# A graph-network stack on one core: min tiles on GpSimd in place of sums, all other tiles on ScalarE, products in column groups

## The chip, the cores and the metric

The kernel runs on one core of a Trainium2 chip. The time is the device time of that core in microseconds, the median of several executions. The profile is of one execution of its own. Engines are named as the profile names them: PE (TensorE matmuls), PEld (its weight loads), DVE (VectorE), ACT (ScalarE), POOL (GpSimd) and SP (SyncE).

## The reference, cut to what matters

Four layers follow each other on 64 independent graphs of 256 nodes with 128 features each, all in float32; one 256 x 256 matrix `adj` serves as adjacency and as weights. Each layer takes `h = relu(layernorm(x))` and adds its result to `x`: five steps of a gated recurrence, a two-hop polynomial filter, a normalised graph convolution, and an attention layer. The attention layer is what the change is about:

```python
W1, W2 = (W[:, :F], W[:, F:])                 # W is adj
s1 = jnp.einsum('bkf,ef->bke', x, W1)
s2 = jnp.einsum('bkf,ef->bke', x, W2)
pre = s1[:, :, None, :] + s2[:, None, :, :] + b_lin
h = jnp.where(pre >= 0, pre, ALPHA * pre)      # ALPHA = 0.2
e = jnp.einsum('bije,e->bij', h, a) + bias     # bias is adj
attn = jax.nn.softmax(e, axis=2)
out = jax.nn.sigmoid(jnp.einsum('bij,bjf->bif', attn, x))
```

For each graph this asks for 256 x 256 x 256 values of `h`, reduced over the last axis with the weights `a`. The leaky relu is split into `0.2 * pre` and `0.8 * relu(pre)`. The first part is linear, and its half that depends on `i` alone drops out of the softmax; the other half is one matrix product. The second part has to be made element by element. It can be made as `relu(s1 + s2)`, or as `max(s2, -s1)`, which differs from it by `s1` and so by something that is constant in a row of the softmax; `-min(-s2, s1)` is the same value again.

## The kernel before

The graphs go in 32 pairs (`NB = 2`, `p`). Each pair has a front (`front`, all layers up to the projections of the attention layer), 64 slots of score work, and two tails (`tail`, softmax and output of 128 rows each).

In slot `n` the kernel works on four rows `i` of both graphs (rows `r`, `r+32`, `r+64`, `r+96` of one 128-row half `ic`), for each of the two halves `k` of the 256 features. It makes one tile per `k`: 128 features x (4 rows x 2 graphs x 256 nodes `j`). Then `scores(n)` multiplies both tiles on PE with a sliding window of the weights (`win`), so that row `r` of each 32-row group of a PSUM bank gets its sum; each tile takes four 512-wide matmuls, one in each of the four 32-column groups of the array. One such matmul is two instructions in the profile[...].

Who makes the tiles:

- `k = 0`: DVE, one `tensor_tensor` with `max` over the whole tile (`rl_v`, L620). It reads `s2a` in PSUM (`banks[0]`) and `s1n` (negated) in SBUF, both broadcast.
- `k = 1`, two slots of three (kind "g"): POOL adds `s2b` and `s1b` over the whole tile (`rl_g`, L608, in `make_sum`), and ACT then takes the relu in place (L625).
- `k = 1`, the third slot (kind "s"): ACT alone, eight relu activations of 128 x 256 with `s1b` as pointer bias (`rl_s`, L635), reading a copy of `s2b` in PSUM (`s2p`, `banks[1]`).

`make(n + 4)` issues the tiles of DVE and ACT four slots ahead of their scores, `make_sum(n + 7)` the sums seven slots ahead. Buffers: 5 for `rl_v`, 6 for `rl_g`, 2 for `rl_s`. At the first tile of a pair, `make` projects `s2a` anew into `banks[0]` on PE; this overwrites what the tiles of the pair before read.

The front's and the tail's operations run between the slots. They are generators that yield before each step, and `background(n)` takes steps from them by their due times. A planner keeps a clock for each engine: `ran(engine, us, *after)` books a price for every piece of work, and the prices decide where a step is put. `in_order` then fixes each engine's program order as it was issued. A front begins two pairs ahead of its slots. The front's products with features as the contracted axis come in two forms: `side_by_side` issues four matmuls with 32 weight columns each, one for each column group; `project_token` (L295) and the last product of `tail` (L564) use one matmul with all 128 columns. Norms take their statistics on DVE, invert the root on POOL (`inverse_root`, L253 and L254), negate and scale the mean there (L326, L327), and apply both on ACT (L331).

Of the kernel before, what the change touches and what calls it, by code (L numbers as in the profile page):

```python
# [19 lines left out]
ALPHA = 0.2  # L20
PE, DVE, ACT, POOL = ENGINES = (mybir.EngineType.PE, mybir.EngineType.DVE, mybir.EngineType.Activation, mybir.EngineType.Pool)
AHEAD = 4
SUM_AHEAD = 7
SLOTS = 64


# [1 line left out]
def kernel(  # L28
# [47 lines left out]

    nc = tc.nc  # L80
    B, N, D = x.shape
    NC = N // P
# [6 lines left out]
    relu_pool = ctx.enter_context(tc.tile_pool(name="relu", bufs=3))  # L89
    psum = ctx.enter_context(tc.tile_pool(name="psum", bufs=1, space=PSUM))  # L90
    banks = [psum.tile([P, NB * N], F32, name=f"bank{k}") for k in range(8)]
    s2a, s2p = (b.rearrange("p (b n) -> p b n", b=NB) for b in banks[:2])
    pes = banks[2:4]


# [3 lines left out]
    def ran(engine, us, *after):  # L99
        clock[engine] = max(clock[engine], 0.0, *after) + us  # L100
        return clock[engine] + SEEN[engine]
# [131 lines left out]
        nc.scalar.dma_start(acol[:, k:k + 1], a_vec[k * P:(k + 1) * P].rearrange("(p o) -> p o", o=1))  # L233
    win = const.tile([P, NE, 63], F32, name="win")
    nc.vector.memset(win, 0.0)
    a_rep = const.tile([P, NE, P], F32, name="a_rep")
    nc.vector.memset(a_rep, 1.0)
    nblin = const.tile([P, NE], F32, name="nblin")
    nc.vector.tensor_scalar(nblin, blin, -1.0, None, op0=OP.mult)
    for k in range(NE):  # L240
        nc.vector.tensor_scalar(win[:, k, 31:32], acol[:, k:k + 1], 1.0 - ALPHA, None, op0=OP.mult)
        nc.vector.tensor_scalar(a_rep[:, k, :], a_rep[:, k, :], acol[:, k:k + 1], None, op0=OP.mult)

    pt = bank([P, P], "pt")
# [44 lines left out]
    def project_token(pp, pairs):  # L289

        pp = by_token(pp)
        for b in range(NB):
            for c in range(NC):
                for k, (t, w) in enumerate(pairs):
                    nc.tensor.matmul(pp[:, b, c, :], t[:, b, c * P:(c + 1) * P], w,  # L295
                                     start=(k == 0), stop=(k == len(pairs) - 1))

    def feat(name, **kw):
        return work.tile([P, NB, N], F32, name=name, **kw)
# [7 lines left out]
    SHORT = dict(tag="short", bufs=14)  # L307


    PROJECT, MIX, TURN, PRODUCT, PRODUCTS = 0.86, 1.74, 0.69, 1.18, 2.99  # L310
    COPY, BIASED, TANH, ELEMENTS = 0.48, 0.58, 0.57, 0.61

    def norm(src, since, h):

        stats = work.tile([P, NB * NC, 6], F32, name="stats")
        mv = work.tile([P, NB * NC, 2], F32, name="mv")
        s, h = rows_of(src), rows_of(h)
        yield DVE, since
        for k in range(NB * NC):
            nc.vector.bn_stats(stats[:, k, :], s[:, k, :])  # L320
        for k in range(NB * NC):
            nc.vector.bn_aggr(mv[:, k, :], stats[:, k, :])
        t = ran(DVE, 1.04, since)
        yield POOL, t
        inverse_root(mv[:, :, 1], OP.add, LN_EPS)
        nc.gpsimd.tensor_scalar(mv[:, :, 0], mv[:, :, 0], -1.0, None, op0=OP.mult)  # L326
        nc.gpsimd.tensor_mul(mv[:, :, 0], mv[:, :, 0], mv[:, :, 1])  # L327
        t = ran(POOL, 1.6, t)
        yield ACT, t
        for k in range(NB * NC):  # L330
            nc.scalar.activation(h[:, k, :], s[:, k, :], AF.Relu, bias=mv[:, k, 0:1], scale=mv[:, k, 1:2])  # L331
        return ran(ACT, 1.54, t)
# [6 lines left out]
        spare.append([bank[0], t])  # L339
        return c, t  # L340

    KEPT = {"hT": dict(bufs=4), "hT3": {}, "s2b": {}}

    READY = {}

    def front(p):
# [160 lines left out]
        hT, t_hT = copied("hT3", b, t)  # L507
        yield PE, t_hT, 1
        b = take()
        project(b[0], adj_t[:, 1, P:2 * P], hT)  # L510
        t = ran(PE, PROJECT, t_hT, b[1])
        yield ACT, t
        s2b, t_2 = copied("s2b", b, t)
        yield PE, t_hT, 1
        b = take()
        project(b[0], adj_t[:, 0, P:2 * P], hT)
# [8 lines left out]
        project(b[0], adj_t[:, 0, 0:P], hT)  # L525
        t = ran(PE, PROJECT, t_hT, b[1])
        yield ACT, t
        s1n = feat("s1n")
        nc.scalar.activation(s1n, by_feature(b[0]), AF.Identity, bias=nblin[:, 0:1], scale=-1.0)
        t_n = ran(ACT, BIASED, t)  # L530
        spare.append([b[0], t_n])
        READY[p] = dict(x3=x3, h3=h3, hT=hT, s1n=s1n, s1b=s1b, s2b=s2b, t_b=max(t_b, t_2), t_n=t_n)

    def tail(p, ic, pe, since, x3, h3):

# [25 lines left out]
        po = b[0][:, :NB * D].rearrange("p (b d) -> p b d", b=NB)  # L561
        for k in range(NB):
            for c in range(NC):
                nc.tensor.matmul(po[:, k, :], wT[:, k, c, :], h3[:, k, c, :], start=(c == 0), stop=(c == NC - 1))  # L564
        t = ran(PE, PRODUCT, t, b[1])
        yield DVE, t_s
        rs = work.tile([P, NB], F32, name="rs")
# [15 lines left out]

    TILES = {}
    t_pe = {}
    t_free = {"v": [0.0] * 5, "g": [0.0] * 6, "s": [0.0] * 2}
    TAILED = set()

    def where(n):
        return n // SLOTS, n % SLOTS // 32, n % 32  # L590

    def kind(n):
        return "s" if n % 3 == 0 else "g"

    def operands(n, s1, s2):

        _, ic, r = where(n)
        i0 = ic * P + r
        whole = [P, 4, NB, N]
        rows = s1[:, :, i0:i0 + 97:32].rearrange("p b g -> p g b").unsqueeze(3)  # L600
        return s2.unsqueeze(1).to_broadcast(whole), rows.to_broadcast(whole)

    def make_sum(n):
        if n >= NPAIR * SLOTS or kind(n) != "g":
            return
        ops = READY[where(n)[0]]
        tile_ = relu_pool.tile([P, 4, NB, N], F32, name="rl_g", bufs=6)
        nc.gpsimd.tensor_add(tile_, *operands(n, ops["s1b"], ops["s2b"]))  # L608
        TILES[n, 1] = tile_, ran(POOL, 3.58, ops["t_b"], t_free["g"].pop(0))

    def make(n):
        if n >= NPAIR * SLOTS:
            return
        p, ic, r = where(n)
        ops = READY[p]
        if "t_2a" not in ops:
            project(banks[0], adj_t[:, 1, 0:P], ops["hT"])
            ops["t_2a"] = ran(PE, PROJECT, clock[DVE] + SEEN[DVE])
        tile_ = relu_pool.tile([P, 4, NB, N], F32, name="rl_v", bufs=5)
        nc.vector.tensor_tensor(tile_, *operands(n, ops["s1n"], s2a), op=OP.max)  # L620
        TILES[n, 0] = tile_, ran(DVE, 2.2, ops["t_2a"], ops["t_n"], t_free["v"].pop(0))
        if kind(n) == "g":
            tile_, since = TILES[n, 1]
            t = tile_.rearrange("p g b n -> p (g b n)")
            nc.scalar.activation(t, t, AF.Relu)  # L625
            TILES[n, 1] = tile_, ran(ACT, 1.8, since)
        else:
            if "t_2p" not in ops:
                nc.scalar.copy(s2p, ops["s2b"])
                ops["t_2p"] = ran(ACT, COPY, ops["t_b"])  # L630
            tile_ = relu_pool.tile([P, 4, NB, N], F32, name="rl_s", bufs=2)
            for g in range(4):
                for b in range(NB):
                    i = ic * P + g * 32 + r
                    nc.scalar.activation(tile_[:, g, b, :], s2p[:, b, :], AF.Relu,  # L635
                                         bias=ops["s1b"][:, b, i:i + 1], scale=1.0)
            TILES[n, 1] = tile_, ran(ACT, 2.86, t_free["s"].pop(0))

    def scores(n):
        p, ic, r = where(n)  # L640
        pe = pes[ic % 2]
        if r == 0:
            project(pe, g2, READY[p]["hT"], stop=False)
            ran(PE, PROJECT, t_pe.get(p * NC + ic - 2, 0.0))
        for k in range(NE):
            tile_, since = TILES.pop((n, k))

            for g in range(4):
                nc.tensor.matmul(pe[g * 32:(g + 1) * 32, :], win[:, k, 31 - r:63 - r], flat(tile_[:, g]),  # L649
                                 start=False, stop=(r == 31 and k == NE - 1), skip_group_check=True)  # L650
            t_free["v" if k == 0 else kind(n)].append(ran(PE, PROJECT, since))

    CHAINS = {}

# [37 lines left out]

    def background(n):
        p, k = n // SLOTS, n % SLOTS + 1
        room = SLOTS - SUM_AHEAD - 3
        while True:
            todo = []
            for key in CHAINS:
                if isinstance(key, tuple):
                    late = 2.0  # L700
                else:

                    due = total * (0.5 * (min(1.0, k / room) + 1) if key == p + 1 else 0.5 * k / SLOTS)
                    late = due - CHAINS[key][2]
                todo.append((-late, key))
            for late, key in sorted(todo, key=lambda x: x[0]):
                late = -late
                if late < -AHEAD_STEPS:
                    continue
                wait = wait_of(key)  # L710
                if wait <= TOLERANCE or late > LATE and wait < 100 or key == p + 1 and k >= room:
                    break
            else:
                return
            advance(key)

    AHEAD_STEPS, TOLERANCE, LATE = 15, 0.05, 8

    for n in range(SUM_AHEAD):
        make_sum(n)  # L720
    for n in range(AHEAD):
        make(n)
    in_order()
    for n in range(NPAIR * SLOTS):
        if n % SLOTS == 0:
            begin_front(n // SLOTS + 2)
        background(n)
        make_sum(n + SUM_AHEAD)
        make(n + AHEAD)
        scores(n)  # L730
        in_order()
        if n % 32 == 31:
            p, ic, _ = where(n)
            begin((p, ic), tail(p, ic, pes[ic % 2], clock[PE] + SEEN[PE], READY[p]["x3"], READY[p]["h3"]))
# [33 lines left out]
```

## Time and profile before

| | us |
|---|---|
| three runs | 5563.02, 5567.29, 5567.29 |
| median | 5567.29 |
| profiled execution, its own time | 5561.99 |
| span of the profiled execution | 5560.2 |
| first score matmul starts | 149.2 |
| last score matmul ends | 5549.3 |

Up to 149 us the kernel sets up its constants and runs the fronts of the first two pairs; the 2048 slots follow, and the last tail ends the program. Over the span PE is busy for 96%, DVE 95%, ACT 97% and POOL 94%; the mean granted PE clock is 0.989. DMA carries 25.9 MB at a mean of 5 GB/s.

A line of the page's groups has the line of the kernel, the engine, the operation, output and inputs by name with their shapes, the count, the busy time of the group, the mean nanoseconds of one, and the idle time of the engine just before them with what ended most of it. Consecutive instructions of an engine overlap, so the mean duration of one is longer than the distance from one start to the next. A line of the waits has the waiting engine, tile and line, what it waited for, the total microseconds, the number of times and the longest. A line of the timeline has start, length, engine, line, operation and count, merged over like instructions. "Seam" is used below for the place where the slots of one pair end and those of the next begin.

### The profile page before, as it was taken

The page shows a single profiled execution, that of the slowest core. Times are in us where ns is not written, and L with a number is a line of the kernel's source. Part 1 is how long each engine was busy: PE and PEld are TensorE (multiplying, and loading weights), DVE is VectorE, ACT ScalarE, POOL GpSimd, SP SyncE. Part 2 cuts the span into 40 slices and gives each one's busy share as a digit, 9 for nine tenths or more (in the row PEclk, how much of TensorE's full clock was granted, in tenths as well). Part 3 has the DMA queues.
Part 4 walks back from the last instruction along what each step waited for, and adds up shares of the span by engine and source line. Part 5 has one row for each costly group of instructions (what it writes and reads, how often), then busy time and mean ns, then how long its engine had stood idle before and what let it go on. Part 6 is the DMA issues. An engine that isn't in the chain of part 4 may idle for free.

```text
span 5560.2 us, 122022 instructions
## 1 busy us (share of the span) xinstructions
PE 5364.9 (96%) x51733; PEld 1876.4 (34%) x51733; DVE 5273.8 (95%) x4224; ACT 5390.2 (97%) x8910; POOL 5222.9 (94%) x2075
## 2 busy tenths in 40 slices
PE   7999999999999999999999999999999999999998
PEld 3333333333333333333333333333333333333322
DVE  3989999999999999999999999999999999999998
ACT  3999999999999999999999999999999999999998
POOL 1999999999999999999999999999999999999998
PEclk9999999999999999999999999999999999999999
DMA  0000000000000000000000000000000000000000
GB/s 20 2 4 5 5 2 5 5 4 5 4 3 5 4 5 5 2 5 5 4 5 4 3 5 4 5 5 2 5 5 4 5 4 3 5 2 3 3 2 4
DMA packets 38741, 25.91 MB, mean 5 GB/s; under 512 B 3504, under 2 KB 38192, under 8 KB 38192
## 3 DMA queue, kind: packets, MB, share of 16 engines
q1 hardware_dynamic: 35088, 17.05, 1.0%
q8 instruction: 404, 6.62, 0.5%
q10 hardware_dynamic: 3104, 1.05, 0.1%
q14 instruction: 145, 1.19, 0.1%
HBM read 9.70 MB, written 8.39 MB: 3 GB/s over the span
## 4 chain that ended last, share of the span: by engine, by line
PE 56%; DVE 20%; ACT 16%; issue 6%; POOL 2%; DMA 0%; ACTq 0%; DVEq 0%; POOLq 0%; SPq 0%
PE bank L649 35%; DVE rl_v L620 16%; PE bank L259 16%; ACT rl_g L625 7%; ACT rl_s L635 6%; POOL rl_g L608 2%; PE bank L295 2%; PE bank L287 2%; PE bank L564 1%; ACT h L331 1%; DVE bank L404 1%; PE bank L280 1%; DVE d L400 1%; DVE hT L408 1%; DVE stats L320 0%
## 5 line engine op out<-in xcount | busy, mean ns | idle before, releaser
L608 POOL TENSOR_TENSOR rl_g<-s2b,s1b 128x2048 f32<-128x2048 f32 x1365 | 4901.1, 3626 | 147.6 <-PE bank L649 133.5
L620 DVE TENSOR_TENSOR rl_v<-bank,s1n 128x2048 f32<-128x2048 f32 x2048 | 4576.9, 2280 | 151.9 <-PE bank L649 89.8
L625 ACT ACTIVATE rl_g<-rl_g 128x2048 f32<-128x2048 f32 x1365 | 2846.3, 2198 | 19.0 <-POOL rl_g L608 18.7
L635 ACT ACTIVATE rl_s<-bank,s1b 128x256 f32<-128x256 f32 x5464 | 2226.4, 730 | 41.2 <-PE bank L649 40.1
L649 PE MATMUL bank<-rl_v,win 128*32 128x512 f32 x16384 | 2187.9, 599 | 12.0 <-DVE rl_v L620 11.6
L649 PE MATMUL bank<-rl_g,win 128*32 128x512 f32 x10920 | 1434.4, 595 | 14.3 <-ACT rl_g L625 14.3
L649 PEld LDWEIGHTS bank<-rl_v,win 128*32 128x32 f32 x16384 | 514.1, 110 | 1068.2 <-issue 933.2
L649 PE MATMUL bank<-rl_s,win 128*32 128x512 f32 x5464 | 754.5, 595 | 0.5 <-ACT rl_s L635 0.5
L649 PEld LDWEIGHTS bank<-rl_g,win 128*32 128x32 f32 x10920 | 352.5, 111 | 858.4 <-issue 710.6
L649 PEld LDWEIGHTS bank<-rl_s,win 128*32 128x32 f32 x5464 | 190.2, 110 | 439.5 <-issue 374.2
L259 PE MATMUL bank<-adj_t,h 128*32 128x256 f32 x5120 | 309.5, 382 | 7.4 <-ACT h L419 7.4
L259 PE MATMUL bank<-hT,adj_t 128*32 128x512 f32 x1024 | 149.0, 662 | 105.4 <-DVE rl_v L620 104.6
L259 PEld LDWEIGHTS bank<-adj_t,h 128*32 128x32 f32 x5120 | 156.2, 110 | 156.0 <-ACT h L419 34.8
L331 ACT ACTIVATE h<-x,mv 128x128 f32<-128x128 f32 x384 | 166.5, 581 | 11.8 <-POOL mv L327 11.7
L259 PE MATMUL bank<-mT,w 128*32 128x512 f32 x1280 | 168.3, 592 | 0.0
L259 PE MATMUL bank<-mT,w5t 128*32 128x512 f32 x1280 | 168.3, 592 | 0.0
L259 PE MATMUL bank<-rh,u5t 128*32 128x512 f32 x1280 | 168.2, 592 | 0.0
L395 ACT ACTIVATE bank<-bank,gate_b 128x512 f32<-128x512 f32 x160 | 156.5, 978 | 11.6 <-PE bank L259 11.2
L259 PE MATMUL bank<-hT,u3t 128*32 128x512 f32 x1280 | 166.7, 593 | 0.0
L259 PE MATMUL bank<-mT,w4t 128*32 128x512 f32 x1280 | 166.7, 592 | 0.0
L377 ACT ACTIVATE bank<-bank,gate_b 128x512 f32<-128x512 f32 x160 | 152.1, 951 | 13.2 <-PE bank L259 13.0
L381 DVE SCALAR_TENSOR_TENSOR rh<-bank,hT 128x512 f32<-128x512 f32 x160 | 109.3, 683 | 56.7 <-ACT bank L377 55.7
(111 smaller groups left out, 3458.7 us busy)
## 6 DMA issues: line engine op xcount, KB each, us to landing
xin<-in_x_dram SPq DMA_DIRECT2D x64, 128.0 KB, 2.2
out_dram<-o SPq DMA_DIRECT2D x64, 128.0 KB, 1.8
w_raw<-in_L_gnn_w_w_dram ACTq DMA_DIRECT2D x3, 128.0 KB, 2.6
th_raw<-in_L_gnn_Theta_dram ACTq DMA_DIRECT2D x1, 320.0 KB, 3.3
adj_n<-in_adj_dram SPq DMA_DIRECT2D x1, 256.0 KB, 5.0
w_raw<-in_L_gnn_u_w_dram ACTq DMA_DIRECT2D x2, 64.0 KB, 2.2
bias<-in_L_gnn_bias_dram ACTq DMA_DIRECT2D x2, 64.0 KB, 3.4
w<-in_L_gnn_weight_dram ACTq DMA_DIRECT2D x1, 64.0 KB, 3.0
```

The costliest lines, as they stand in the source:

```text
L259: nc.tensor.matmul(o[g:g + 32], w[:, g:g + 32], t, start=start, stop=stop, skip_group_check=True)
L287: nc.tensor.transpose(pt[:, b, c, :], ht[:, b, c * P:(c + 1) * P], ident)
L295: nc.tensor.matmul(pp[:, b, c, :], t[:, b, c * P:(c + 1) * P], w, start=(k == 0), stop=(k == len(pairs) - 1))
L331: nc.scalar.activation(h[:, k, :], s[:, k, :], AF.Relu, bias=mv[:, k, 0:1], scale=mv[:, k, 1:2])
L377: nc.scalar.activation(r[0], pr[0], AF.Tanh, bias=br, scale=0.5)
L381: nc.vector.scalar_tensor_tensor(rh, by_feature(r[0]), 1.0, hT, op0=OP.add, op1=OP.mult)
L395: nc.scalar.activation(pv[0], pv[0], AF.Tanh, bias=bh, scale=1.0)
L608: nc.gpsimd.tensor_add(tile_, *operands(n, ops["s1b"], ops["s2b"]))
L620: nc.vector.tensor_tensor(tile_, *operands(n, ops["s1n"], s2a), op=OP.max)
L625: nc.scalar.activation(t, t, AF.Relu)
L635: nc.scalar.activation(tile_[:, g, b, :], s2p[:, b, :], AF.Relu, bias=ops["s1b"][:, b, i:i + 1], scale=1.0)
L649: nc.tensor.matmul(pe[g * 32:(g + 1) * 32, :], win[:, k, 31 - r:63 - r], flat(tile_[:, g]), start=False, stop=(r == 31 and k == NE - 1), s ...
```

## The change

GpSimd no longer makes sums. It makes whole tiles: for 5 of every 16 slots the `k = 1` tile is eight `tensor_scalar` instructions of 128 x 256 with `min` of `s2n` (the negated projection) and a pointer scalar out of `s1b`. All other `k = 1` tiles come from ScalarE, as eight relu activations with scale -1 on `s2n`. In one slot of 32 ScalarE makes the `k = 0` tile as well; in the others DVE makes it, now as `min` of `s1a` and the negated projection in `banks[0]`. Tiles made by `min` are multiplied with `win_n`, the window with its sign turned. Buffers are 5 for "v", 3 for "m" and 5 for "s". The products of `project_token` and of the tail go through `side_by_side`. The negation of the mean in `norm` moves from POOL to DVE. Four of the planner's prices change, and `M_US` is a new one.

```diff
-SUM_AHEAD = 7
+EARLY = 7
+M_OF_16, M_US = 5, 7.3
...
+    win_n = const.tile([P, NE, 63], F32, name="win_n")
+    nc.vector.memset(win_n, 0.0)
+    w2n = const.tile([P, N], F32, name="w2n")
+    nc.vector.tensor_scalar(w2n, adj_t[:, 1, :], -1.0, None, op0=OP.mult)
...
-    nblin = const.tile([P, NE], F32, name="nblin")
-    nc.vector.tensor_scalar(nblin, blin, -1.0, None, op0=OP.mult)
...
+        nc.vector.tensor_scalar(win_n[:, k, 31:32], acol[:, k:k + 1], ALPHA - 1.0, None, op0=OP.mult)
...
-                    nc.tensor.matmul(pp[:, b, c, :], t[:, b, c * P:(c + 1) * P], w,
-                                     start=(k == 0), stop=(k == len(pairs) - 1))
+                    side_by_side(pp[:, b, c, :], t[:, b, c * P:(c + 1) * P], w, k == 0, k == len(pairs) - 1)
...
-    PROJECT, MIX, TURN, PRODUCT, PRODUCTS = 0.86, 1.74, 0.69, 1.18, 2.99
+    PROJECT, MIX, TURN, PRODUCT, PRODUCTS = 0.86, 1.74, 0.69, 0.88, 2.64
...
-        t = ran(DVE, 1.04, since)
+        nc.vector.tensor_scalar(mv[:, :, 0], mv[:, :, 0], -1.0, None, op0=OP.mult)
+        t = ran(DVE, 1.12, since)
         yield POOL, t
         inverse_root(mv[:, :, 1], OP.add, LN_EPS)
-        nc.gpsimd.tensor_scalar(mv[:, :, 0], mv[:, :, 0], -1.0, None, op0=OP.mult)
         nc.gpsimd.tensor_mul(mv[:, :, 0], mv[:, :, 0], mv[:, :, 1])
-        t = ran(POOL, 1.6, t)
+        t = ran(POOL, 1.4, t)
...
-                nc.tensor.matmul(po[:, k, :], wT[:, k, c, :], h3[:, k, c, :], start=(c == 0), stop=(c == NC - 1))
+                side_by_side(po[:, k, :], wT[:, k, c, :], h3[:, k, c, :], c == 0, c == NC - 1)
...
-    def kind(n):
-        return "s" if n % 3 == 0 else "g"
+    def kind(n, k):
+        if k == 0:
+            return "s" if n % 32 == 7 else "v"
+        return "m" if n * M_OF_16 % 16 < M_OF_16 else "s"
...
-        nc.gpsimd.tensor_add(tile_, *operands(n, ops["s1b"], ops["s2b"]))
-        TILES[n, 1] = tile_, ran(POOL, 3.58, ops["t_b"], t_free["g"].pop(0))
+        for g in range(4):
+            for b in range(NB):
+                i = ic * P + g * 32 + r
+                nc.gpsimd.tensor_scalar(t[:, g, b, :], ops["s2n"][:, b, :], ops["s1"][1][:, b, i:i + 1], None, op0=OP.min)
+        TILES[n, 1] = t, ran(POOL, M_US, ops["t_1"][1], ops["t_2"], free)
...
-        if "t_2a" not in ops:
-            project(banks[0], adj_t[:, 1, 0:P], ops["hT"])
+        if "t_s2" not in ops:
+            project(banks[0], w2n[:, 0:P], ops["hT"])
+            nc.scalar.copy(s2[1], ops["s2n"])
...
-        nc.vector.tensor_tensor(tile_, *operands(n, ops["s1n"], s2a), op=OP.max)
...
-            nc.scalar.activation(t, t, AF.Relu)
-            TILES[n, 1] = tile_, ran(ACT, 1.8, since)
...
+            if kind(n, k) == "v":
+                nc.vector.tensor_tensor(t, *operands(n, ops["s1"][0], s2[0]), op=OP.min)
+                TILES[n, k] = t, ran(DVE, 2.2, since)
+            else:
+                for g in range(4):
+                    for b in range(NB):
+                        i = ic * P + g * 32 + r
+                        nc.scalar.activation(t[:, g, b, :], s2[k][:, b, :], AF.Relu,
+                                             bias=ops["s1"][k][:, b, i:i + 1], scale=-1.0)
+                TILES[n, k] = t, ran(ACT, 2.86, since)
...
-                nc.tensor.matmul(pe[g * 32:(g + 1) * 32, :], win[:, k, 31 - r:63 - r], flat(tile_[:, g]),
+                nc.tensor.matmul(pe[g * 32:(g + 1) * 32, :], w[:, k, 31 - r:63 - r], flat(t[:, g]),
```

`w` is `win` for tiles of kind "s" and `win_n` for the others. In `front`, `s2b` becomes `s2n` (projected with `w2n`), and `s1n` becomes `s1a` (bias `blin`, scale 1).

More of the change, by code (lines that the diff above doesn't have):

```diff
@@ L91 @@
     banks = [psum.tile([P, NB * N], F32, name=f"bank{k}") for k in range(8)]
-    s2a, s2p = (b.rearrange("p (b n) -> p b n", b=NB) for b in banks[:2])
+    s2 = [b.rearrange("p (b n) -> p b n", b=NB) for b in banks[:2]]
     pes = banks[2:4]
@@ L340, in copied @@
         return c, t
-    KEPT = {"hT": dict(bufs=4), "hT3": {}, "s2b": {}}
+    KEPT = {"hT": dict(bufs=4), "hT3": {}, "s2n": {}}
     READY = {}
@@ L509, in front @@
         b = take()
-        project(b[0], adj_t[:, 1, P:2 * P], hT)
+        project(b[0], w2n[:, P:2 * P], hT)
         t = ran(PE, PROJECT, t_hT, b[1])
         yield ACT, t
-        s2b, t_2 = copied("s2b", b, t)
+        s2n, t_2 = copied("s2n", b, t)
         yield PE, t_hT, 1
@@ L527, in front @@
         yield ACT, t
-        s1n = feat("s1n")
-        nc.scalar.activation(s1n, by_feature(b[0]), AF.Identity, bias=nblin[:, 0:1], scale=-1.0)
+        s1a = feat("s1a")
+        nc.scalar.activation(s1a, by_feature(b[0]), AF.Identity, bias=blin[:, 0:1], scale=1.0)
         t_n = ran(ACT, BIASED, t)
         spare.append([b[0], t_n])
-        READY[p] = dict(x3=x3, h3=h3, hT=hT, s1n=s1n, s1b=s1b, s2b=s2b, t_b=max(t_b, t_2), t_n=t_n)
+        READY[p] = dict(x3=x3, h3=h3, hT=hT, s1=(s1a, s1b), s2n=s2n, t_1=(t_n, t_b), t_2=t_2)
     def tail(p, ic, pe, since, x3, h3):
@@ L585 @@
     t_pe = {}
-    t_free = {"v": [0.0] * 5, "g": [0.0] * 6, "s": [0.0] * 2}
+    t_free = {"v": [0.0] * 5, "m": [0.0] * 3, "s": [0.0] * 5}
     TAILED = set()
@@ L600, in operands, with new_tile, make_early @@
         rows = s1[:, :, i0:i0 + 97:32].rearrange("p b g -> p g b").unsqueeze(3)
-        return s2.unsqueeze(1).to_broadcast(whole), rows.to_broadcast(whole)
-    def make_sum(n):
-        if n >= NPAIR * SLOTS or kind(n) != "g":
-            return
-        ops = READY[where(n)[0]]
-        tile_ = relu_pool.tile([P, 4, NB, N], F32, name="rl_g", bufs=6)
-        nc.gpsimd.tensor_add(tile_, *operands(n, ops["s1b"], ops["s2b"]))
-        TILES[n, 1] = tile_, ran(POOL, 3.58, ops["t_b"], t_free["g"].pop(0))
+        return rows.to_broadcast(whole), s2.unsqueeze(1).to_broadcast(whole)
+    def new_tile(n, k):
+        which = kind(n, k)
+        t = relu_pool.tile([P, 4, NB, N], F32, name="rl_" + which, bufs={"v": 5, "m": 3, "s": 5}[which])
+        return t, t_free[which].pop(0)
+    def make_early(n):
+        if n >= NPAIR * SLOTS or kind(n, 1) != "m":
+            return
+        p, ic, r = where(n)
+        ops = READY[p]
+        t, free = new_tile(n, 1)
+        for g in range(4):
[3 more added lines that the diff above has]
+        TILES[n, 1] = t, ran(POOL, M_US, ops["t_1"][1], ops["t_2"], free)
     def make(n):
@@ L615, in make @@
         ops = READY[p]
-        if "t_2a" not in ops:
-            project(banks[0], adj_t[:, 1, 0:P], ops["hT"])
[L618 to L625, printed above, removed]
-            TILES[n, 1] = tile_, ran(ACT, 1.8, since)
[L627 to L637, printed above, removed]
+        if "t_s2" not in ops:
+            project(banks[0], w2n[:, 0:P], ops["hT"])
+            nc.scalar.copy(s2[1], ops["s2n"])
+            ops["t_s2"] = (ran(PE, PROJECT, clock[DVE] + SEEN[DVE], clock[ACT] + SEEN[ACT]),
+                           ran(ACT, COPY, ops["t_2"]))
+        for k in range(NE):
+            if kind(n, k) == "m":
+                continue
+            t, free = new_tile(n, k)
+            since = max(ops["t_s2"][k], ops["t_1"][k], free)
+            if kind(n, k) == "v":
[8 more added lines that the diff above has]
+                TILES[n, k] = t, ran(ACT, 2.86, since)
     def scores(n):
@@ L645, in scores @@
         for k in range(NE):
-            tile_, since = TILES.pop((n, k))
+            t, since = TILES.pop((n, k))
+            which = kind(n, k)
+            w = win if which == "s" else win_n
             for g in range(4):
-                nc.tensor.matmul(pe[g * 32:(g + 1) * 32, :], win[:, k, 31 - r:63 - r], flat(tile_[:, g]),
+                nc.tensor.matmul(pe[g * 32:(g + 1) * 32, :], w[:, k, 31 - r:63 - r], flat(t[:, g]),
                                  start=False, stop=(r == 31 and k == NE - 1), skip_group_check=True)
-            t_free["v" if k == 0 else kind(n)].append(ran(PE, PROJECT, since))
+            t_free[which].append(ran(PE, PROJECT, since))
     CHAINS = {}
@@ L694, in background @@
         p, k = n // SLOTS, n % SLOTS + 1
-        room = SLOTS - SUM_AHEAD - 3
+        room = SLOTS - EARLY - 3
         while True:
@@ L717 @@
     AHEAD_STEPS, TOLERANCE, LATE = 15, 0.05, 8
-    for n in range(SUM_AHEAD):
-        make_sum(n)
+    for n in range(EARLY):
+        make_early(n)
     for n in range(AHEAD):
@@ L727 @@
         background(n)
-        make_sum(n + SUM_AHEAD)
+        make_early(n + EARLY)
         make(n + AHEAD)
```

## The prediction

> **What bounds the kernel now.** I read the busy shares first, then the costliest groups, the table of waits, the timeline at the seam between two pairs, and last the chain. The chain (PE 56%, DVE 20%, ACT 16%) passes between engines, and the page gives four of them within three points of each other, so neither names a bound alone:
>
> ```profile
> PE 5364.9 (96%) x51733; PEld 1876.4 (34%) x51733; DVE 5273.8 (95%) x4224; ACT 5390.2 (97%) x8910; POOL 5222.9 (94%) x2075
> ...
> L608 POOL TENSOR_TENSOR rl_g<-s2b,s1b 128x2048 f32<-128x2048 f32 x1365 | 4901.1, 3626 | 147.6 <-PE bank L649 133.5
> L620 DVE TENSOR_TENSOR rl_v<-bank,s1n 128x2048 f32<-128x2048 f32 x2048 | 4576.9, 2280 | 151.9 <-PE bank L649 89.8
> L625 ACT ACTIVATE rl_g<-rl_g 128x2048 f32<-128x2048 f32 x1365 | 2846.3, 2198 | 19.0 <-POOL rl_g L608 18.7
> L635 ACT ACTIVATE rl_s<-bank,s1b 128x256 f32<-128x256 f32 x5464 | 2226.4, 730 | 41.2 <-PE bank L649 40.1
> ```
>
> Seen here: four tile-making groups keep three engines busy, and a tile costs an engine much the same either way. Mean durations overlap, so I take the spacing of consecutive starts in the trace where an engine runs without a wait: L635 0.357 us (eight make a tile: 2.86), L625 1.80, L620 2.20, L608 3.60, eight score matmuls 0.858. The timeline shows two of them, ten sums in 36.02 us and five maxima in 11.07:
>
> ```profile
> 2497.44 36.02 POOL L608 TENSOR_TENSOR rl_g<-s2b,s1b 128x2048 f32<-128x2048 f32 x10
> 2499.69 11.07 DVE L620 TENSOR_TENSOR rl_v<-bank,s1n 128x2048 f32<-128x2048 f32 x5
> ...
> 2518.01 1.89 PE L259 MATMUL bank<-hT,adj_t 128*32 128x512 f32 x8 [3.67 <-DVE rl_v L620]
> ...
> 2519.66 1.95 PE L649 MATMUL bank<-rl_v,win 128*32 128x512 f32 x8
> ```
>
> The last two lines are the seam: PE stands 3.67 us until VectorE has made the old pair's last tile, then works at about half rate for some microseconds (1.95 us where other sets show 1.04). Between such stalls PE has few gaps. They return every 169.5 us (24 seams from 992.3 to 5062.0 us), the pair's period. The table of waits gives them in total:
>
> ```profile
> POOL rl_g L608 <- PE bank L649: 133.5, 71, 4.5
> ...
> PE bank L259 <- DVE rl_v L620: 104.6, 31, 4.5
> ...
> DVE rl_v L620 <- PE bank L649: 89.8, 87, 2.6
> DVE rl_v L620 <- PE bank L259: 59.1, 31, 10.9
> ```
>
> Work of one pair, in microseconds out of 169.5:
> - ACT 166.1: 42.7 relus x 1.80 = 76.8, 21.3 eight-piece tiles x 2.86 = 61.0, and 28.3 else (16 copies x 0.47, 15 tanh x 0.57, 16 norms x 0.385, 6.1 for exp, outputs and the rest).
> - DVE 165: 64 x 2.20 = 140.7 plus 24.
> - POOL 164.9: 42.7 x 3.60 = 153.6 plus 11.3.
> - PE 164.1: 128 x 0.858 = 109.8; five steps of a mix (1.73) and five projections (0.86) = 30.1; three mixes 5.2; six projections 5.1; ten transposes with their surroundings x 0.72 = 7.2; token products 6.7.
>
> ACT is the longest by a point; the 3.4 us above it are what coupling through queues and buffers loses. A single cut would move the bound to the next engine at most; a gain needs all four cut.
>
> [...] L620 (one input in PSUM) holds 2.2 us beside an unbroken row of sums. [...] eight full-width product matmuls between scores add 1.22 us, though their own spacing is 0.111. [...] No run so far shows two readers of banks[0].
>
> **The change, part by part** (per pair).
>
> *Sums go.* GpSimd loses 42.7 sums (-153.6) and makes 5 of 16 k=1 tiles whole: 20 tiles, eight tensor_scalar(min) of 128x256 each. No row has a pointer scalar. From below, the immediate form of this shape:
>
> ```profile
> L577 POOL TENSOR_SCALAR o<-o x64: 401/408/420, 261.4 to 5556.0; 128x256 f32<-128x256 f32 x64
> L578 POOL TENSOR_TENSOR o<-o,x x64: 723/738/752, 261.9 to 5556.5; 128x256 f32<-128x256 f32 x64
> ```
>
> Eight at 0.408 are 3.3 us. [...] From above, the two-input form 0.738 plus the 0.312 between starts of a small dependent tensor_scalar: 1.05, or 8.4 us a tile. The diff's planner books 7.3 (0.91 each). Its other prices (3.58, 1.80, 2.20, 2.86) match the spacings above within 1%, so I take 7.3, ends 3.3 and 8.4. POOL: 20 x 7.3 + 11.3 - 1.1 (four negations of 0.28 leave) = 156.2.
>
> *ScalarE* loses 76.8 of relus and makes 44 + 2 tiles in place of 21.3: 46 x 2.86 = 131.6, plus 28.3 = **159.9** (-6.2). That is 368 short instructions a pair against 171; the 0.357 already holds within runs of eight. It also stops waiting for sums (18.7 us in all). scale=-1 is an immediate either way: nothing, for the spacing is set by the same form. The copy into s2[1] moves from the first "s" tile to the pair's first tile: same count, nothing.
>
> *VectorE* loses 2 of 64 tiles (-4.4) and gains four 4-element negations, booked 0.08: 0.3. **160.9**. Bounds: the negation could [...] wait for GpSimd's current instruction, mean half of 0.91, so up to 1.8 a pair; the two ACT tiles now read banks[0] with it, at worst slowing one maximum each by half, 2.2. I take zero for both, for the range 4. max to min and swapped inputs: same shape, one SBUF operand, nothing.
>
> *Products in groups.* The sixteen layer products and eight tail products per pair cost 3 x 1.22 + 3.01 = 6.7. [...] Mix matmuls of 256 columns run 32 in 1.73; 128 columns scaled by width give 0.86 per four products, so 3 x 0.86 + 2.59 = 5.2: -1.5. If spacing doesn't fall below 0.054 a matmul, 24 x 8 x 0.054 = 10.4: +3.7. I take -1.5. PE: **162.6**.
>
> *Waits moved.* A norm step on POOL now queues behind a tile of 7.3 instead of 3.6; five visits per front make at most 18 us, hidden because fronts start two pairs ahead (339 us). Without that cover every engine would stand at the seam. Three buffers for min tiles last 9.6 slots, 25 us, against 7.3 to make one: no wait. SP's loads and stores, and every DMA, are unchanged. Setup gains four small VectorE operations of 0.15 to 0.3 us and loses one: under 1 us in all, uncovered.
>
> *The seam stays in the code*: the s2[0] projection still waits for the old pair's last VectorE tile. Its cause shrinks: VectorE was as loaded as PE (165 against 164.1) and is now 1.7 below, so more of its five buffers are full when PE arrives. I expect 2.4 us of seam and coupling on 162.6, where before it was 5.4 on 164.1, and so PE as the bound at **165.0**.
>
> Sum: 4.5 x 32 = 144 off the profiled span of 5560.2 gives 5416; with 1.8 around it, as before, 5418. The runs' median, 5567.3, lies 5.3 above the profiled 5562.0: **5423**.
>
> **Rivals.**
> 1. *The seam stands* (0.11). PE still loses 5.4 a pair because VectorE's background is bunched there: 168.0, -1.5 x 32 = -48, 5519. For: the wait is structural. Against: VectorE gets 4.1 us lighter.
> 2. *VectorE gets the bound* (0.05) through both collisions: 160.9 + 4 + 3.4 = 168.3, 5529. For: both readers and the negation are new. Against: each overlap is short.
> 3. *GpSimd's pointer form is too dear* (0.12). From a tile of about 7.8 us on, 20 tiles and 10.2 else exceed 166 and the period grows: at 8.4, 168 + 10.2 + 3.4 = 181.6, +12.1 x 32 = +387: 5954, slower. For: nothing in the trace shows a pointer scalar, and 7.3 leaves 6%. Against: the planner's other prices are right.
> 4. *Group products cost more* (0.03): PE 167.8 + 3.4 = 171.2, +54: 5621.
> A change that doesn't do what it says would be a planner whose order is so off that tiles come late; it looks like rival 1.
>
> **How the numbers follow.** The forecast (0.69) has its own range of 5350 (seam nearly gone, 162.8) to 5490. Adding rivals 1 and 2 takes the range to 5335 to 5560; rivals 3 and 4 stay outside, 0.15, and a little below. A measurement here can tell about 0.2%, 11 us, from no change. Faster 0.83 (forecast and most of 1 and 2), within 0.02, slower 0.15.
>
> **What would show each step.** POOL's tensor_scalar rows near 0.91 us apart and its share near 93%; ACT's eight-piece spacing still 0.357 and its share below 98%; PE highest; eight product sets at 0.86; the seam wait under 60 us in all. Wrong: POOL at 98% with PE waiting for min tiles, seam waits above 100 us, or L620's successor over 2.3 us.

## The result, and the profile after

The changed kernel takes 5977.24 us (median of 4 runs, 5976.11 to 5979.06) against 5566.51 for the kernel before: a ratio of 1.0739, 95% interval 1.0721 to 1.0758. The forecast was 5423 us, faster. The change makes the kernel 411 us slower.

The page of the changed kernel, engine shares first, then the groups that answer to those shown of before (columns as there):

```profile
PE 5422.4 (91%) x56341; PEld 1890.3 (32%) x56341; DVE 5187.4 (87%) x4291; ACT 5237.3 (88%) x13857; POOL 4892.9 (82%) x5702
...
L623 POOL TENSOR_SCALAR rl_m<-s2n,s1b 128x256 f32<-128x256 f32 x5120 | 4595.0, 918 | 469.4 <-PE bank L664 405.7
L642 DVE TENSOR_TENSOR rl_v<-s1a,bank 128x2048 f32<-128x2048 f32 x1984 | 4429.8, 2279 | 356.6 <-ACT rl_s L648 163.5
L648 ACT ACTIVATE rl_s<-bank,s1b 128x256 f32<-128x256 f32 x11264 | 4393.0, 798 | 42.4 <-PE bank L664 41.4
...
L648 ACT ACTIVATE rl_s<-bank,s1a 128x256 f32<-128x256 f32 x512 | 193.5, 489 | 556.6 <-DVE rl_v L642 556.6
...
L290 PE MATMUL bank<-ident,sc 128*128 128x128 f32 x256 | 72.9, 436 | 427.8 <-ACT sc L549 427.8
```

No engine is full: the highest share is 91%, where before all four stood at 94 to 97%. The work is done about as priced (2279 ns for a VectorE tile, 2280 before; 918 ns for a min instruction, of which eight were booked at 7.3 us), so the tiles are not what became dear: every engine waits. Two idle columns stand out. ScalarE's few k=0 tiles (512 instructions, 64 tiles) waited 556.6 us for VectorE; before, there were none. PE's transposes of the softmax waited 427.8 us for ScalarE's exp, and the same transposes before waited 2.2 us:

```profile
L287 PE MATMUL bank<-ident,sc 128*128 128x128 f32 x256 | 42.2, 287 | 2.2 <-ACT sc L547 2.2
```

The table of waits of the changed kernel gives the number and the longest of each:

```profile
ACT rl_s L648 <- DVE rl_v L642: 556.6, 64, 9.8
...
PE bank L290 <- ACT sc L549: 427.8, 60, 7.9
...
POOL rl_m L623 <- PE bank L664: 405.7, 233, 8.4
...
DVE rl_v L642 <- ACT rl_s L648: 163.5, 65, 3.2
DVE rl_v L642 <- PE bank L664: 148.5, 97, 3.7
...
PE bank L262 <- DVE rl_v L642: 25.8, 31, 6.9
```

There are 64 waits for 64 tiles: each of them waits, 8.7 us on average. The seam, by contrast, fell from 104.6 to 25.8 us. The timeline around one such tile shows how the waits follow from each other (idle time before an instruction stands in brackets):

```profile
2523.35 5.77 ACT L648 ACTIVATE rl_s<-bank,s1b 128x256 f32<-128x256 f32 x15
...
2533.62 1.04 PE L664 MATMUL bank<-rl_m,win_n 128*32 128x512 f32 x8
...
2535.41 2.28 DVE L642 TENSOR_TENSOR rl_v<-s1a,bank 128x2048 f32<-128x2048 f32 x1
...
2537.78 3.02 ACT L648 ACTIVATE rl_s<-bank,s1a 128x256 f32<-128x256 f32 x8 [8.65 <-DVE rl_v L642]
...
2540.64 0.56 ACT L549 ACTIVATE sc<-sc,nmx 128x256 f32<-128x256 f32 x1
2540.83 4.48 DVE L642 TENSOR_TENSOR rl_v<-s1a,bank 128x2048 f32<-128x2048 f32 x2 [1.89 <-ACT rl_s L648]
...
2541.34 1.18 PE L290 MATMUL bank<-ident,sc 128*128 128x128 f32 x4 [6.67 <-ACT sc L549]
...
2542.44 1.94 PE L664 MATMUL bank<-rl_v,win_n 128*32 128x512 f32 x8
```

ScalarE has run ahead of VectorE and stops. It resumes only when the VectorE minimum that stands before its tile in the program has ended (2535.41 + 2.28 = 2537.69). VectorE's next minimum then waits for ScalarE's tile. The exp of the tail stands right behind that tile in ScalarE's order, PE's transpose waits for the exp with all scores queued behind it, and after 6.67 us of standing PE runs at half rate (1.94 us for eight matmuls instead of 1.04); PE's mean granted clock in this kernel is 0.953, before 0.989.

No data passes between the two engines there. Both read `banks[0]`. In the program as built, each of the 64 ScalarE tiles carries a wait on VectorE's semaphore, and the VectorE minimum behind it one on ScalarE's (the table shows 65 waits of that kind). The tile starts 34 to 116 ns after the end of the minimum ahead of it, and the minimum behind it 32 to 34 ns after the tile's end, at all 64 places. Before, no tile of ScalarE read `banks[0]`. The two reads of one PSUM tile by two engines have been put in order, as if one of them were a write.

### The profile page after: what moved, and what is told of

Same layout as the page of the kernel before. It is cut to its first block, busy times and chain, and to the rows that moved or that the text cites. A ratio compares the mean times of both kernels' runs of the same rounds, so it can differ in the third digit from the quotient of the medians.

```text
span 5975.9 us, 139181 instructions
## 1 busy us (share of the span) xinstructions
PE 5422.4 (91%) x56341; PEld 1890.3 (32%) x56341; DVE 5187.4 (87%) x4291; ACT 5237.3 (88%) x13857; POOL 4892.9 (82%) x5702
## 4 chain that ended last, share of the span: by engine, by line
DVE 45%; PE 37%; issue 7%; ACT 5%; POOL 2%; ACTq 0%; POOLq 0%; DVEq 0%
DVE rl_v L642 36%; PE bank L664 19%; PE bank L262 15%; ACT rl_s L648 4%; POOL rl_m L623 2%; PE bank L290 2%; DVE stats L322 1%; DVE bank L406 1%; DVE hT L410 1%; DVE d L402 1%; PE bank L283 1%; DVE rh L383 1%; DVE nmx L544 1%; DVE sc L540 1%; DVE x L496 1%
## 5 line engine op out<-in xcount | busy, mean ns | idle before, releaser
L623 POOL TENSOR_SCALAR rl_m<-s2n,s1b 128x256 f32<-128x256 f32 x5120 | 4595.0, 918 | 469.4 <-PE bank L664 405.7
L642 DVE TENSOR_TENSOR rl_v<-s1a,bank 128x2048 f32<-128x2048 f32 x1984 | 4429.8, 2279 | 356.6 <-ACT rl_s L648 163.5
L648 ACT ACTIVATE rl_s<-bank,s1b 128x256 f32<-128x256 f32 x11264 | 4393.0, 798 | 42.4 <-PE bank L664 41.4
L664 PE MATMUL bank<-rl_v,win_n 128*32 128x512 f32 x15872 | 2112.0, 602 | 24.2 <-DVE rl_v L642 23.7
L664 PE MATMUL bank<-rl_s,win 128*32 128x512 f32 x11776 | 1565.7, 603 | 0.0
L664 PEld LDWEIGHTS bank<-rl_v,win_n 128*32 128x32 f32 x15872 | 494.2, 111 | 1008.1 <-issue 811.7
L648 ACT ACTIVATE rl_s<-bank,s1a 128x256 f32<-128x256 f32 x512 | 193.5, 489 | 556.6 <-DVE rl_v L642 556.6
L664 PE MATMUL bank<-rl_m,win_n 128*32 128x512 f32 x5120 | 676.3, 593 | 3.4 <-POOL rl_m L623 3.2
L664 PEld LDWEIGHTS bank<-rl_s,win 128*32 128x32 f32 x11776 | 385.9, 112 | 892.7 <-issue 861.2
L290 PE MATMUL bank<-ident,sc 128*128 128x128 f32 x256 | 72.9, 436 | 427.8 <-ACT sc L549 427.8
L664 PEld LDWEIGHTS bank<-rl_m,win_n 128*32 128x32 f32 x5120 | 167.5, 110 | 395.4 <-issue 343.7
```

The source lines that it names most:

```text
L290: nc.tensor.transpose(pt[:, b, c, :], ht[:, b, c * P:(c + 1) * P], ident)
L623: nc.gpsimd.tensor_scalar(t[:, g, b, :], ops["s2n"][:, b, :], ops["s1"][1][:, b, i:i + 1], None, op0=OP.min)
L642: nc.vector.tensor_tensor(t, *operands(n, ops["s1"][0], s2[0]), op=OP.min)
L648: nc.scalar.activation(t[:, g, b, :], s2[k][:, b, :], AF.Relu, bias=ops["s1"][k][:, b, i:i + 1], scale=-1.0)
L664: nc.tensor.matmul(pe[g * 32:(g + 1) * 32, :], w[:, k, 31 - r:63 - r], flat(t[:, g]), start=False, stop=(r == 31 and k == NE - 1), skip_gr ...
```

## The experiments

**Theory W**: this order between two readers of `banks[0]`, amplified by the tail's exp behind it, is the cost. **Rivals**: the min tiles of GpSimd come late (G), ScalarE's many short instructions cost more than their spacing shows (I), and reads of two engines in one bank slow each other (C). Later a question about the products in column groups came up: is it the order that their new prices lead to that costs time (O), or the group products themselves (P)? Times are medians; each ratio is to the kernel before on the same chip.

| kernel | us | ratio, 95% interval |
|---|---|---|
| changed kernel | 5977.24 | 1.0739 (1.0721 to 1.0758) |
| e1_v_all | 5630.57 | 1.0116 (1.0099 to 1.0133) |
| e2_own_copy | 5476.36 | 0.9840 (0.9825 to 0.9854) |
| e3_moved | 5659.31 | 1.0168 (1.0153 to 1.0183) |
| e4_groups_only | 5583.00 | 1.0032 (1.0020 to 1.0044) |
| e5_one_read | 6030.18 | 1.0835 (1.0819 to 1.0851) |
| e6_seam_dve | 5450.38 | 0.9790 (0.9775 to 0.9804) |
| e7_seam_full | 5415.71 | 0.9730 (0.9714 to 0.9747) |
| e8_groups_full_order | 5404.05 | 0.9710 (0.9694 to 0.9726) |
| e9_full_groups_order | 5461.64 | 0.9814 (0.9800 to 0.9829) |
| e10_groups_old_prices | 5551.73 | 0.9977 (0.9970 to 0.9983) |
| e11_copy_old_order | 5477.52 | 0.9842 (0.9827 to 0.9856) |
| e12_before_one_read | 5858.36 | 1.0526 (1.0509 to 1.0544) |

### Taking the second reader away

**e1_v_all**: VectorE makes every k=0 tile.

```diff
-            return "s" if n % 32 == 7 else "v"
+            return "v"
```

> The changed kernel, but VectorE makes every k=0 tile again (none on ScalarE), so banks[0] has one reader. Theory W (ScalarE's k=0 tile is made to wait for VectorE's last read of banks[0], and VectorE's next for ScalarE, and the tail's exp stands behind it): the 556 us of ScalarE waits and the 428 us of PE waits for exp go; VectorE is longest with 64 x 2.20 + 24.6 = 165.3 us a pair, with 3.4 of coupling about 5540 us, between 5470 and 5570. Theory G (GpSimd's min tiles come too late or hold up the norms): stays above 5850 us, POOL waits and PE's waits for rl_m as now. Theory I (ScalarE's short instructions cost more than their spacing shows): stays above 5850, since 1408 of 1472 such tiles remain.

5630.57 us: 347 faster than the changed kernel with only 64 of ScalarE's 1472 tiles moved off it, which speaks against G and I. But it is 90 us above the 5540 expected, and above the stated 5570. Its waits:

```profile
ACT rl_s L648 <- PE bank L664: 309.4, 181, 8.8
...
PE bank L262 <- DVE rl_v L642: 130.0, 31, 6.6
```

The waits between ScalarE and VectorE are gone. ScalarE now idles 309 us for buffers, and PE stands 130 us at the seam, more than the 104.6 before: VectorE, the longest at 165.3 us of work a pair, gets a period of 169.5 + (5630.57 - 5566.28) / 32 = 171.5. The coupling is 6.2 a pair, not the 3.4 I carried over from before. What makes up the other 2.8 is not separated here.

**e2_own_copy**: the ScalarE tiles stay where they are and read an SBUF copy of their own. `front` makes the projection that fills `banks[0]` once more and copies it to SBUF as `s2m`, as it does with `s2n`; the setup's buffers `w_raw` and `w_sum` go from 3 to 2 and from 2 to 1.

```diff
+        b = take()
+        project(b[0], w2n[:, 0:P], hT)
...
+        s2m, t_m = copied("s2m", b, t)
...
+                src = s2[1] if k else ops["s2m"]
...
-                        nc.scalar.activation(t[:, g, b, :], s2[k][:, b, :], AF.Relu,
+                        nc.scalar.activation(t[:, g, b, :], src[:, b, :], AF.Relu,
```

> The changed kernel, with ScalarE's k=0 tiles kept in place but reading an SBUF copy of their own: one more projection (0.86 us PE) and copy (0.47 us ScalarE) per pair, no second reader of banks[0]; two setup buffers are one smaller each to make room. Theory W: the waits between ScalarE and VectorE go, and PE at 163.5 us a pair plus 2.4 gives about 5450 us, between 5390 and 5520, faster than the kernel without tiles on ScalarE. Theory G and theory I: above 5850 us.

5476.36 us: 501 us below the changed kernel, with 1.3 us more work a pair. The lines of its page and of its waits:

```profile
PE 5305.6 (97%) x56597; PEld 1860.6 (34%) x56597; DVE 5189.7 (95%) x4291; ACT 5269.7 (96%) x13889; POOL 4892.2 (89%) x5702
```

```profile
POOL rl_m L629 <- PE bank L671: 387.1, 237, 5.7
...
PE bank L262 <- DVE rl_v L648: 58.4, 31, 6.9
```

PE is the highest again, GpSimd has room (89%) and waits mostly for buffers, and the seam costs 58.4 us. This is close to the profile that the prediction described (GpSimd was to stand near 93%), with the change's tiles, counts and engines otherwise untouched. G and I are out.

**e3_moved**: the same wait, elsewhere.

```diff
-            return "s" if n % 32 == 7 else "v"
+            return "s" if n % 32 == 20 else "v"
```

> The changed kernel with ScalarE's k=0 tile at row 20 of 32 in place of row 7, so that its wait doesn't stand ahead of a tail's exp. Theory W with the tail as the amplifier: ScalarE still waits for VectorE 64 times, 250 to 550 us in all, PE's 428 us of waits for exp fall below 60, and the time falls to between 5550 and 5750 us. Theory W without amplifier (the lost ScalarE time alone is the cost, 8.7 x 2 on 159.9 us a pair = 177): about 5850 to 5980 us. Theory G or I: 5950 to 6000 us, unchanged.

5659.31 us, inside the band for the amplifier. ScalarE's waits, at 239.1 us, come out a little under the 250 stated. The table:

```profile
ACT rl_s L648 <- DVE rl_v L642: 239.1, 63, 5.0
...
PE bank L262 <- ACT h L421: 122.1, 60, 5.3
...
PE bank L290 <- ACT sc L549: 5.5, 3, 2.8
```

PE's wait for the exp falls from 427.8 to 5.5 us. ScalarE still waits 63 times, and PE now waits 122.1 us for a front's copy `h`, which ScalarE makes soon after the tile. So of the 501 us between the changed kernel and e2, 318 go with the place ahead of the tail's exp, and 183 remain with the tile at row 20. No third place was tried.

### One element is enough

**e5_one_read**: e2 with a read of `banks[0]` that does no useful work.

```diff
+                if k == 0:
+                    nc.scalar.copy(one, s2[0][:, 0, 0:1])
```

> The kernel e2_own_copy with one more ScalarE instruction ahead of each of its k=0 tiles: a copy of a single element per partition out of banks[0], whose result nobody uses (64 such copies[...]). Theory W (the order between two engines reading one PSUM bank is the cost, whatever the amount read): ScalarE waits for VectorE at 57 to 64 places again, PE waits for the tail's exp again, and the time returns to between 5900 and 6030 us. Theory C (it is the collision of 2048 reads in one bank, or the tile's work, that costs): 5475 to 5500 us.

6030.18 us, at the upper edge of theory W's band and 0.2 us past it (6029.38 to 6031.93 over the runs):

```profile
ACT one L654 <- DVE rl_v L649: 586.1, 64, 10.3
...
PE bank L291 <- ACT sc L556: 441.2, 60, 8.2
```

64 reads of one element per partition bring both waits back and cost 554 us. C is out: what counts is not the amount read, but that a second engine reads.

**e12_before_one_read**: the same in the kernel before.

```diff
         TILES[n, 0] = tile_, ran(DVE, 2.2, ops["t_2a"], ops["t_n"], t_free["v"].pop(0))
+        if n % 32 == 7:
+            nc.scalar.copy(one, s2a[:, 0, 0:1])
```

> The kernel before, unchanged but for one ScalarE copy of a single element per partition out of banks[0] in one slot of 32 (row 7), right after that slot's VectorE maximum; nobody uses it. [...] Theory W (an engine that reads a PSUM bank in the middle of another's reads is made to wait, and the tail's exp behind it): ScalarE waits 64 times for 2 to 9 us and the time rises by 130 to 450 us, to 5690 to 6020. If the wait hurts only beside the other parts of the change: 5565 to 5590 us.

5858.36 us, 292 above the kernel before and in theory W's band. The wait needs no other part of the change:

```profile
ACT one L624 <- DVE rl_v L621: 274.1, 59, 7.5
...
PE bank L281 <- ACT h L332: 96.0, 21, 5.6
```

What stands behind the wait here is not the exp that had been expected (PE waits 6.8 us for it) but a front's norm `h`, for which PE waits 96.0 us. What the wait delays is what comes soon after it in ScalarE's order: the exp in the changed kernel, the copy `h` in e3, the norm's `h` here.

Whether the chip needs this order was not tried; the wait alone was not taken out of a program.

### The products and the seam

**e4_groups_only**: the kernel before with `side_by_side` in `project_token` and `tail`, and the two prices 0.88 and 2.64.

> The kernel before, with the products of project_token and the tail in column groups alone, and the planner's two prices for them. PE loses 1.5 us of work a pair (48 us in all) if eight group products take 0.86 us. If the kernel before is bound by ScalarE at 166.1 us a pair, little of it shows: 5540 to 5570 us. If PE with its seam is the bound, all of it: about 5520 us. If the group products are dear, slower: up to 5690.

5583.00 us, slower by 17. Of the three readings only the last, dear group products, allows a slower kernel, and the trace rules it out: four products between scores add 0.87 us instead of 1.22, and twelve add 2.62 instead of 3.01, as forecast. PE got less work and the kernel lost time.

**e6_seam_dve**: e2 with `banks[0]` filled by VectorE.

```diff
-            project(banks[0], w2n[:, 0:P], ops["hT"])
+            nc.vector.tensor_copy(s2[0], ops["s2m"])
```

> The kernel e2_own_copy, with banks[0] filled at the seam by a VectorE copy of the SBUF projection instead of a second projection on PE: PE loses 0.86 us a pair and never waits at the seam, VectorE gains one copy of 128x512, some 0.6 us. If the seam is what is left over above PE's work: PE at 162.6 us a pair plus 1 to 2 of coupling gives 5390 to 5420 us, with PE's waits for VectorE at the projection (58 us and the slow matmuls behind it) gone. If VectorE (161.5 us a pair) with its own coupling of 3.4 is the bound: about 5440. If the seam cost nothing: 5450 to 5476.

5450.38 us, 26 below e2. PE's wait at the projection is gone, but the time is 30 us above the band of the case that PE alone is left and 10 above the one that VectorE binds. It falls at the edge of the third case, that the seam cost nothing (5450 to 5476), so this run alone does not tell what the seam was worth. **e7_seam_full**: e6 with both products full width and the prices 1.18 and 2.99.

> The kernel e6_seam_dve with the products back in full-width matmuls (and the planner's two old prices). If products in groups save PE 1.5 us a pair and PE is the bound there: 35 to 50 us slower than e6_seam_dve. If the saving was never real: the same as e6_seam_dve within 11 us.

5415.71 us: faster by 35, the opposite of what was expected. But two things differ between e6 and e7: the form of the products, and the planner's prices for them, which change the order of the instructions on the engines. The two were therefore crossed. **e8_groups_full_order** has group products and the old prices, **e9_full_groups_order** full-width products and the new prices; the built order on ScalarE, VectorE and GpSimd is that of e7 and of e6. **e10_groups_old_prices** does for e4 what e8 does for e6.

> The kernel e6_seam_dve (products in column groups) with the planner's two old prices, so that the order of the instructions on ScalarE, VectorE and GpSimd is that of e7_seam_full; only the form of the products differs from e7. Theory O (the order that the two prices lead to made e6 slower than e7, the group products themselves save PE time): at or below e7's 5416, down to 5370 us. Theory P (the group products themselves are dear): at e6's 5450 us.

> The kernel e7_seam_full (products full width) with the planner's two new prices, so that the order is that of e6_seam_dve; only the form of the products differs from e6. Theory O: slower than e6, 5450 to 5500 us. Theory P: near e7, 5416 us.

> The kernel before with products in column groups, like e4_groups_only, but with the planner's two old prices, so that the order on the other engines is that of the kernel before. Theory O: no slower than the kernel before, 5520 to 5567 us. Theory P: slower than the kernel before, at e4's 5583 us.

| | order of the new prices | order of the old prices |
|---|---|---|
| rebuilt seam, full width | 5461.64 (e9) | 5415.71 (e7) |
| rebuilt seam, groups | 5450.38 (e6) | 5404.05 (e8) |
| kernel before, groups | 5583.00 (e4) | 5551.73 (e10) |

Theory O holds in these three. The group products gain 11 to 12 us in either order, and 13 in the kernel before (5564.80 there). (e6 and e7 ran on another chip than e8 and e9, but the kernel before differs by only 0.8 us between the two.) The order that the new prices lead to costs 46 us at the rebuilt seam and 31 in the kernel before. In the kernel before it shows at the seam (waits of e4, then of e10):

```profile
PE bank L259 <- DVE rl_v L619: 143.8, 31, 6.3
```

```profile
PE bank L259 <- DVE rl_v L619: 106.5, 31, 4.6
```

The new prices are the truer ones for the new products, so "truer" is not what makes an order good; why this one is worse in these places stays open. e8 is the fastest kernel of all, 2.9% under the kernel before. Its page:

```profile
PE 5268.6 (98%) x56341; PEld 1850.8 (34%) x56341; DVE 5195.2 (96%) x4323; ACT 5258.3 (97%) x13889; POOL 4890.8 (91%) x5702
```

**e11_copy_old_order**: e2 with the old prices.

> The kernel e2_own_copy (seam projection still on PE, products in column groups) with the planner's two old prices for the products. Theory O, as measured between e6 and e8 (46 us by the order alone): 5420 to 5440 us, which is where the prediction had put the change. If the order mattered only at the rebuilt seam: 5465 to 5485 us, like e2.

5477.52 us, within 1.2 of e2, not the 5420 to 5440 of theory O. In this kernel the order makes no difference. That it still has the projection on PE at the seam cannot be the whole reason, since the kernel before has it too and lost 31 us by the order. So neither the order nor the seam has a fixed price: with the new prices the rebuilt seam is worth 26 us (e2 to e6), with the old ones 73 (e11 to e8).

## Why the prediction was wrong

**The step that failed** is in the part on VectorE: "the two ACT tiles now read banks[0] with it, at worst slowing one maximum each by half, 2.2. I take zero for both". I had seen the new second reader, and priced it as two reads that slow each other, an estimate with no trace behind it. What it brings is a wait, and a wait is priced by who stands behind it. Between the changed kernel and e2 it is 501 us, 15.7 us a pair, seven times the upper end. The question not asked was: how far ahead of VectorE does ScalarE run when it reaches row 7 of 32, and what is next in its order? In the changed kernel the answers are 8.7 us on average and the tail's exp, with PE behind it. The prediction also gave three signs of being wrong, and none of them came (GpSimd stood at 82%, the seam took 25.8 us in all, the minimum 2.20 us), for none of them looked for a wait of this kind.

**What such a slowing would cost was not measured.** In the changed kernel the two engines never read `banks[0]` at once: none of ScalarE's 512 instructions on it overlaps a minimum of VectorE, and the minima keep their 2.20 us between starts (2.20 before). The cost comes from the wait that the program carries.

**Rival 3 named almost the right time for the wrong reason.** It gave 5954 us from a pointer form at 8.4 us a tile. Measured are 0.895 us between starts, 7.16 a tile, inside the forecast's 7.3, with GpSimd idle for 405.7 us behind PE. Rival 2 named the right place, `banks[0]`, with the wrong price.

**What held.** ScalarE's eight-piece spacing 0.356 (forecast 0.357). VectorE's 2.20 (2.20). Products in groups 0.87 and 2.62 (0.86 and 2.59); what makes them cheaper than the full-width 1.22 and 3.01 is not shown. The seam wait fell under the 60 us that I had set as a mark: 25.8, and 58.4 in e2, where little else stalls. With the second reader gone, e2's period is 169.5 - (5566.28 - 5476.36) / 32 = 166.7 us, on 163.5 us of PE work: 3.2 above it where I had put 2.4. The forecast of 5423 was for a kernel with one projection and one copy fewer than e2; that kernel was never run without the wait. That e8 comes to 5404 does not confirm it: e8 also spares PE the projection at the seam and has the old prices.

**What was sized wrong besides.** The negations took 0.26 us each where 0.08 was booked, 0.7 us a pair more. In the trace they last from 169 to 559 ns. The 24 that met GpSimd at rest last 169 to 172; of the other 104, 52 end 23 to 28 ns behind the end of the GpSimd instruction that ran when they began, and 27 end 247 to 251 ns ahead of it. That fits the wait for GpSimd that was also taken at zero, and it is small. I counted the products' 1.5 us a pair in full because PE was to be the bound. With the order held, 46 us less PE work give 11 to 13 us of time. Where the rest stays was not traced further; a likely reason, not tested, is that PE, VectorE and ScalarE stand within two points of each other in e8, so that a cut on one leaves the next two close behind. And I gave nothing to the planner's prices, although they decide the order, which was worth from 1 us (e2 and e11) to 46 us in these kernels.

## What to carry to other kernels

Before a second engine is set to read a PSUM tile that another engine reads all the time, look at what waits the built program then carries, and give the second engine its own copy: 0.86 us of PE and 0.47 of ScalarE a pair bought back 15.7 here. Price a new wait by the lead of the engine that has to wait and by what is next in its queue, not by the work that it guards. And where a planner's prices fix the order, hold the order when comparing two forms of an instruction, or the order's effect is read as the form's.

## What was not expected of the hardware

The same relu of 128 x 256 with a pointer bias starts every 0.356 us when it reads PSUM (`rl_s<-bank,s1b` in the changed kernel) and every 0.399 us when it reads SBUF (`rl_s<-s2m,s1a` in e2). And a `tensor_scalar` of 128 x 256 on GpSimd takes 918 ns with a pointer scalar (`rl_m`), 2.25 times the 408 ns of the form with two immediates (`o` at L577 before, in place and with other operations); the forecast had bounded it between those 408 and 1050 ns.
